# Two attention layers on one core: layer 1's scores between the halves of its head mixing, column strips for layer 0's row sums, and another order at an image's start

## The chip, the cores and the metric

The kernel runs on one core of one Trainium2 chip. The metric is the device time of one launch in microseconds (us). Before the change it is 4345.27 us, the median of three runs (4342.4 to 4345.67). All data are float32.

## What is computed

Eight images of 512 channels and 32 x 32 positions (T = 1024 tokens) pass two residual layers, each on a group-normalized input. Both layers are attention with 8 heads of 64 channels; layer 1 mixes the heads' scores before the softmax and normalizes the attention map afterwards. Cut to what matters:

```python
# layer 0, x: (8, 512, 1024) after group normalization
q, k, v = split(qkv_w @ groupnorm(x) + qkv_b)          # 8 heads of 64 channels
weight = softmax(einsum('bct,bcs->bts', q * s, k * s))
out = proj_w @ (x + weight @ v) + proj_b

# layer 1
attn = einsum('bhdq,bhdT->bhqT', q, k) * scale
attn = einsum('gh,bhqT->bgqT', w_head, attn)            # mixing of the heads
attn = softmax(attn)
attn = (attn - mean) / sqrt(var + eps) * gamma + beta   # over a head's whole map
out = (attn @ v) @ w_proj.T + b_proj
```

In both layers x = x + layer(groupnorm(x)).

## The kernel before

The program fixes the order of instructions by hand for every engine. Waits and buffers follow from the program: a pool hands out a fixed number of buffers per tag, and a new tile waits until its buffer's last reader is done.

Layer 0 runs image by image (b). In `attention0` 64 steps i go over 8 groups g (a pair of heads, half of the queries) and 8 blocks of keys. A step has `scores` (L982, 64 x 64 tiles of TensorE, four at a time), the exponential on ScalarE (L987), `values` (L1008) and `sums`, which adds up the exponentials on VectorE (L993, L995). After each group `totals` adds them over the keys with a matrix of ones (L1030), two engines copy the two results to a row (L1035, L1036) and two DMAs bring it into 128 partitions. `reciprocals` adds the two parts (L1045), inverts them and spreads them by DMA, and `finish` multiplies (L1068). An `Agenda` holds work for given steps: `totals` comes 2 steps after its group, `reciprocals` 6, `finish` 10 after. The statistics of the next image run beside (L620 and L631 are their small matmuls), and the projections (L856) stand between images.

Layer 1 goes over images again. Within one it goes over 32 half steps x, and 5 more to drain (`half_step`):

- `scores(x, i)`, i = 0, 1 (L1575): 8 matmuls, 16 instructions, of 64 x 64 x 256 into a PSUM tile `s`, copied to `raw` by VectorE (i = 0 and x odd or below 4, L1588) or ScalarE (L1590). Two half steps fill one tile t of `raw`.
- `regroup` (L1599): eight DMAs r of 256 KB per tile t, which put eight heads of one query row beside each other in `re`, in the order R_ORDER. In the steady part each is issued behind the end of a mix or of a values block. Up to half step 4 all are issued at the half step's end. `re` has two halves; one half holds the weights wv for `v_pair` at an image's start.
- `mix(y, j)` with y = x - 4 (L1623): 32 matmuls, 64 instructions, of 64 x 64 x 64 into a PSUM tile `m`, then the exponential (L1629).
- `values(w, i)` with w = x - 5 (L1669): 128 x 64 x 256, summed over a quarter of the image (8 half steps) and taken out by `leave` (L1689, L1691).
- `squares` on ScalarE (L1640), `sum_e` and `sum_e2` on VectorE (L1647, L1651); after each quarter `totals` (L1700) in 32-column strips, `reciprocals`, and `divide` (L1759).

TensorE's order in a half step is scores 0, mix 0, values 0, scores 1, mix 1, values 1. The tiles `s`, `m`, those of the projections and of `v_pair` share one pool of three buffers of two PSUM banks (`m_psum`). `pieces` are DMAs for the next image, one behind each scores block. `v_pair` (L1394) makes two token blocks of v: the image's last two pairs run at the ends of half steps 1 and 2. Each `Projection` (L1319) forms seven products in an ORDER; its `leave` adds them up and calls `finish` for the quarters (0,0), (1,1), (1,0), (0,1) of the result. The first two scores blocks read the upper half of the channels of q, that is quarters (0,0) and (0,1).

Of the kernel before, what the change touches and what calls it, by code (L numbers as in the profile page):

```python
# [9 lines left out]
F32 = mybir.dt.float32  # L10
# [457 lines left out]
def tile_two_attention_layers(  # L468
# [181 lines left out]
    with ExitStack() as l0:  # L650
# [9 lines left out]
        def small_psum(nm):  # L660
            return ps_a.tile([P, FB], F32, tag="small", name=nm)
# [308 lines left out]
        def attention0(b, agenda):  # L970
            q, k, v = q_t[b], k_t[b], v_t[b]
            e, acc, u, zacc, zc, rzb = {}, {}, {}, {}, {}, {}

            def scores(i):

                f, hp, kc = i // (NG * H // 2), i // NG % (H // 2), i % NG
                ps = score_psum(f"s0_{b}_{i}")
                for c in range(2):
                    for m in range(2):
                        r = slice(m * D, m * D + D)  # L980
                        k0 = kc * P + c * D
                        nc.tensor.matmul(  # L982
                            ps[c * D : c * D + D, m], k[r, hp, k0 : k0 + D], q[r, hp, ts(f, FB)],
                            start=True, stop=True,
                        )
                e[i] = epool.tile([P, 2, FB], F32, tag="e", name=f"e0_{b}_{i}")
                nc.scalar.activation(e[i], ps, AF.Exp, scale=S0 * S0)  # L987

            def sums(i):
                g, kc = i // NG, i % NG  # L990
                if kc == 1:
                    zacc[g] = zpool.tile([P, 2, FB], F32, tag="zacc", name=f"zacc_{b}_{g}")
                    nc.vector.tensor_add(zacc[g], e[i - 1], e[i])  # L993
                elif kc > 1:
                    nc.vector.tensor_add(zacc[g], zacc[g], e[i])  # L995

            def values(i):

                g, hp, kc = i // NG, i // NG % (H // 2), i % NG
                if kc == 0:  # L1000
                    acc[g] = [
                        ps_a.tile([P, FB], F32, tag=f"a{a}", name=f"a0_{b}_{g}_{a}", bufs=2 - a)
                        for a in range(2)
                    ]
                for a in range(2):
                    rows = slice(a * D, a * D + D)
                    for m in range(2):
                        nc.tensor.matmul(  # L1008
                            acc[g][a][m * D : m * D + D], v[rows, kc, ts(2 * hp + m, D)],
                            e[i][rows, m], start=(kc == 0), stop=(kc == NG - 1),  # L1010
                        )
                if kc == NG - 1:

                    u[g] = [
                        zpool.tile([P, FB], F32, tag=f"u{a}", name=f"u_{b}_{g}_{a}")
                        for a in range(2)
                    ]
                    for a in (1, 0):
                        nc.scalar.copy(u[g][a], acc[g][a])

            def totals(g):

                z = [
                    ps_a.tile([P, FB], F32, tag="a0", name=f"z_{b}_{g}", bufs=2),
                    small_psum(f"z_{b}_{g}_1"),
                ]
                for a in range(2):
                    rows = slice(a * D, a * D + D)
                    for m in range(2):
                        nc.tensor.matmul(  # L1030
                            z[a][m * D : m * D + D], ones[rows, :D], zacc[g][rows, m],
                            start=True, stop=True,
                        )
                row = zpool.tile([P, 2, FB], F32, tag="row", name=f"row0_{b}_{g}", bufs=1)
                nc.scalar.copy(row[:, 0], z[0])  # L1035
                nc.vector.tensor_copy(row[:, 1], z[1])  # L1036
                zc[g] = stat.tile([P, 2, T // P], F32, tag="zc", name=f"zc_{b}_{g}")
                for a in range(2):
                    nc.sync.dma_start(out=zc[g][:, a], in_=row[0::D, a])

            def reciprocals(g):

                nc.vector.tensor_add(u[g][0], u[g][0], u[g][1])
                zs = stat.tile([P, T // P], F32, tag="zs", name=f"zs_{b}_{g}")
                nc.vector.tensor_add(zs, zc[g][:, 0], zc[g][:, 1])  # L1045
                rz = stat.tile([P, T // P], F32, tag="rz0", name=f"rz_{b}_{g}")
                nc.vector.reciprocal(rz, zs)
                zd = dram.tile([2, FB], F32, tag=f"zd0_{b}_{g}", name=f"zd0_{b}_{g}")
                nc.sync.dma_start(out=zd, in_=rz)
                rzb[g] = zpool.tile([P, FB], F32, tag="rzb", name=f"rzb_{b}_{g}")  # L1050
                for m in range(2):
                    nc.sync.dma_start(
                        out=rzb[g][m * D : m * D + D], in_=zd[m].partition_broadcast(D)
                    )
                col = b * H + g
                junk = stat.tile([P, T // P], F32, tag="junk0", name=f"junkz_{b}_{g}")
                nc.vector.tensor_scalar(
                    junk, zs, 1.0, 0.0, ALU.mult, ALU.add, accum_out=chk[:, 1, col : col + 1]
                )
                r2 = stat.tile([P, T // P], F32, tag="r20", name=f"r2_{b}_{g}")  # L1060
                nc.vector.scalar_tensor_tensor(
                    r2, rz, 1.0 / RZ_MAX, rz, ALU.mult, ALU.mult,
                    accum_out=chk[:, 0, col : col + 1],
                )

            def finish(g):
                hp, f = g % (H // 2), g // (H // 2)
                nc.vector.tensor_mul(u[g][0], u[g][0], rzb[g])  # L1068
                dst = xa_t[b][:, hp, ts(f, FB)]
                nc.vector.tensor_add(dst, dst, u[g][0])  # L1070


            for i in range(0, NI + 2, 2):
                if i < NI:
                    scores(i)
                    scores(i + 1)
                if i >= 2:
                    for w in (i - 2, i - 1):
                        values(w)
                        sums(w)  # L1080
                    if (i - 1) % NG == NG - 1:
                        g = (i - 1) // NG
                        agenda.at(i + 2, lambda g=g: totals(g))
                        agenda.at(i + 6, lambda g=g: reciprocals(g))
                        agenda.at(i + 10, lambda g=g: finish(g))
                agenda.run(i)
                agenda.run(i + 1)
# [61 lines left out]
    with ExitStack() as l1:  # L1149
# [144 lines left out]
                nc.vector.tensor_sub(t[:, i], x, y)  # L1294

        class Projection:
            ORDER = (1, 6, 2, 7, 5, 4, 3)

            def __init__(self, nm, key, n, t, finish, begin=None):

# [257 lines left out]
        class Attention1:  # L1558
# [5 lines left out]
            def scores(self, x, i):  # L1564
# [15 lines left out]
                if x > MLAG:  # L1580
                    self.piece(last)
                if x % 2 and i == 1:
                    self.due = [(t, r) for r in R_ORDER]
                if x % 2 == 0 and i == 0:
                    self.raw[t] = rawpool.tile([P, H, 2, KB], F32, tag="raw", name=f"raw_{b}_{t}")
                dst = self.raw[t][:, 2 * hp : 2 * hp + 2]
# [22 lines left out]
                        behind(dma, ins)  # L1609
                self.pieces = self.pieces[n:]  # L1610

            def mix(self, y, j):

                t, kc = y // 2, y % 2
                if j == 0:
                    self.e[y] = epool.tile([P, 2, T], F32, tag="e", name=f"e1_{self.b}_{y}")
                ps = m_psum(f"m1_{self.b}_{y}_{j}")
                for r in R_ORDER:
                    for c in range(2):
                        k0 = kc * P + c * D  # L1620
                        for a in range(2):
# [4 lines left out]
                                wmix[rows].rearrange("p g i -> p (g i)"),  # L1626
                                start=True, stop=True,
                            )
                nc.scalar.activation(self.e[y][:, j], ps.rearrange("p a c -> p (a c)"), AF.Exp)  # L1629
                self.regroup(last)  # L1630

            def squares(self, y, j):
                if y % QLAG == 0:
# [86 lines left out]
            def reciprocals(self, qb, ag=None, x=None):  # L1720
# [7 lines left out]
                self.rzb = zpool.tile([P, T], F32, tag="rzb", name=f"rzb_{b}_{qb}")  # L1728
                rzb = self.rzb
                spread = [  # L1730
                    lambda two=two: nc.sync.dma_start(
                        out=rzb[two * D : two * D + D], in_=zd[two].partition_broadcast(D)
                    )
                    for two in range(2)
                ]
                if ag is None:
                    for fn in spread:
# [58 lines left out]
            def half_step(self, x, ag):  # L1796
                y, w = x - MLAG, x - MLAG - 1
                first = 0 < w < NX and w % QLAG == 0
                if first:

                    self.scores(x, 0)
                    self.leave(w // QLAG - 1)
# [10 lines left out]
                    self.sum_e2(w, 0)  # L1813
                    self.sum_e2(w, 1)
                if 0 <= y < NX:
                    self.mix(y, 0)
                if 0 <= w < NX:
                    self.values(w, 0)
                if x < NX:
                    self.scores(x, 1)  # L1820
                if 0 <= y < NX:
                    self.mix(y, 1)
                if x <= MLAG or x >= NX:
                    self.regroup(n=NR)
                if x >= NX:
# [28 lines left out]
        for b in range(B):  # L1854
            more = b + 1 < B
            a = Attention1(b)
            ag = Agenda()
            for i in range(NV):
                ag.at(1 + i, lambda i=i: v_pair(b, NV + i))
            free = (NX // 2 - 2 + b) % 2  # L1860
            if more:
                a.pieces += [lambda i=i: y_piece(b + 1, i) for i in range(4 * NCC)]
# [119 lines left out]
```

## Time and profile before

| what | value |
|---|---|
| median of three runs | 4345.27 us |
| the profiled execution | 4355.81 us |
| its span, first to last instruction | 4353.9 us |
| granted TensorE clock | 0.995 |
| TensorE matmuls busy | 4192.3 us |
| VectorE busy | 2911.7 us |
| ScalarE busy | 2329.9 us |
| mix: matmuls, and weight loads | 602.1 us, 585.4 us |
| scores and values of layer 1 | 558.4 us, 558.2 us |
| scores and values of layer 0 | 491.5 us, 485.0 us |
| sums of layer 0 (L1030) | 67.1 us |
| regroup DMAs | 1024 of 256 KB |

The profile lists instructions by line, engine and tile. A row of the timeline has the start and duration in us, the engine, line and operation, the tile written and read, the size (rows * columns of the array that are used, then partitions x elements), and in brackets the idle time before with what ended it; "issue" there means that no wait on another engine is on record. Matmuls overlap, so the distance from one start to the next tells more than a block's duration. PE is TensorE, PEld its weight loads, ACT ScalarE, DVE VectorE, SPq and POOLq the queues of SyncE and GpSimd.

### The profile page before, as it was taken

What the parts mean: (1) busy time and instruction counts of PE and PEld (TensorE: products, weight loads), DVE (VectorE), ACT (ScalarE), POOL (GpSimd) and SP (SyncE); (2) the same over time, 40 slices, a digit from 0 to 9 for tenths busy, and PEclk for the clock granted to TensorE, in tenths of its full rate; (3) what the DMA queues carried; (4) which work ended last, traced back from release to release, by engine and by line L of the source; (5) the groups of instructions that cost most, each with busy time, mean ns of one, the idle gap of its engine ahead of it and who ended that gap; (6) DMA issues with size and microseconds to landing.
All of it is one profiled execution on the core that took longest, in us unless ns stands there. A gap on an engine that the chain in (4) does not pass through costs nothing.

```text
span 4353.9 us, 131477 instructions
## 1 busy us (share of the span) xinstructions
PE 4192.3 (96%) x58568; PEld 2243.2 (52%) x58568; DVE 2911.7 (67%) x3881; ACT 2329.9 (54%) x2730; POOL 53.3 (1%) x86
## 2 busy tenths in 40 slices
PE   7999999999999999799999999999999999999998
PEld 4353535353535353356466466466466466465565
DVE  4748484848484848458668668568577578577577
ACT  1717171717171716158368278277187287286385
POOL 0000000000000000000000000000000000000000
PEclk9999999999999999899999999999999999999999
DMA  4213131212121211257367377277286286375474
GB/s 145 77 54 101 50 104 49 79 49 79 52 76 54 74 49 43 87 140 191 123 166 183 105 187 180 97 195 189 81 202 172 90 206 158 114 199 141 135 175 136
DMA packets 260464, 521.21 MB, mean 120 GB/s; under 512 B 58992, under 2 KB 66544, under 8 KB 253232
## 3 DMA queue, kind: packets, MB, share of 16 engines
q1 hardware_dynamic: 255008, 509.92, 41.8%
q8 instruction: 461, 7.55, 0.8%
q0 software_dynamic: 2576, 0.69, 0.3%
q10 hardware_dynamic: 2304, 2.10, 0.2%
q14 instruction: 115, 0.94, 0.1%
HBM read 196.11 MB, written 46.92 MB: 56 GB/s over the span
## 4 chain that ended last, share of the span: by engine, by line
PE 84%; DVE 6%; DMA 5%; ACT 2%; issue 2%; SPq 1%; POOL 0%; DVEq 0%; ACTq 0%; POOLq 0%
PE a L1669 11%; PE s L1575 11%; PE m L1623 10%; PE s L982 8%; PE a L1008 8%; PE pk L1319 5%; PE pq L1319 4%; PE pp_p L856 4%; PE pv_p L856 4%; PE pv L1394 4%; PE pk_p L856 4%; PE pq_p L856 4%; PE pp L1319 3%; DMA re<-raw 2%; PE t L1700 2%
## 5 line engine op out<-in xcount | busy, mean ns | idle before, releaser
L1623 PEld LDWEIGHTS m<-wmix,re 64*64 64x64 f32 x32768 | 585.4, 135 | 141.9 <-issue 73.7
L1623 PE MATMUL m<-wmix,re 64*64 64x64 f32 x32768 | 602.1, 219 | 44.0 <-issue 34.9
L987 ACT ACTIVATE e<-s 128x1024 f32<-128x1024 f32 x512 | 497.4, 1026 | 235.4 <-PE s L982 235.4
L1629 ACT ACTIVATE e<-m 128x1024 f32<-128x1024 f32 x512 | 528.2, 1032 | 157.7 <-PE m L1623 154.2
L1647 DVE TENSOR_TENSOR z<-z,e 128x1024 f32<-128x1024 f32 x448 | 538.9, 1218 | 69.8 <-ACT e L1629 69.6
L1651 DVE TENSOR_TENSOR z<-z,e 128x1024 f32<-128x1024 f32 x448 | 534.9, 1219 | 74.6 <-ACT e L1640 74.4
L1669 PE MATMUL a<-e,v 128*64 128x256 f32 x4096 | 558.2, 392 | 27.5 <-ACT q L1691 20.9
L1575 PE MATMUL s<-k,q 64*64 64x256 f32 x8192 | 558.4, 388 | 6.2 <-DVE q L1431 4.6
L1590 ACT COPY raw<-s 128x1024 f32<-128x1024 f32 x368 | 372.7, 1015 | 284.4 <-PE s L1575 245.8
L982 PE MATMUL s<-q,k 64*64 64x512 f32 x4096 | 491.5, 594 | 2.3 <-ACT e L987 2.3
L995 DVE TENSOR_TENSOR zacc<-zacc,e 128x1024 f32<-128x1024 f32 x384 | 468.2, 1219 | 28.6 <-ACT e L987 3.9
L1008 PE MATMUL a<-e,v 64*64 64x512 f32 x4096 | 485.0, 589 | 0.0
L1640 ACT ACTIVATE e<-e 128x1024 f32<-128x1024 f32 x448 | 462.1, 1063 | 0.0
L1575 PEld LDWEIGHTS s<-k,q 64*64 64x64 f32 x8192 | 271.5, 132 | 274.5 <-issue 170.7
L1669 PEld LDWEIGHTS a<-e,v 128*64 128x64 f32 x4096 | 250.6, 136 | 155.0 <-issue 24.9
L1008 PEld LDWEIGHTS a<-e,v 64*64 64x64 f32 x4096 | 159.9, 133 | 281.2 <-issue 281.2
L982 PEld LDWEIGHTS s<-q,k 64*64 64x64 f32 x4096 | 156.2, 133 | 281.5 <-issue 257.7
L1588 DVE COPY raw<-s 128x1024 f32<-128x1024 f32 x144 | 176.1, 1223 | 96.3 <-PE s L1575 84.7
L1394 PE MATMUL pv<-re,y 128*128 128x512 f32 x512 | 227.6, 598 | 0.0
L1394 PEld LDWEIGHTS pv<-re,y 128*128 128x128 f32 x512 | 94.8, 190 | 120.1 <-issue 120.1
L1399 DVE COPY v<-pv 128x512 f32<-128x512 f32 x32 | 22.1, 689 | 149.4 <-ACT v L1398 149.4
L856 PE MATMUL pv_p<-left_v,tmp 128*128 128x256 f32 x512 | 115.1, 383 | 4.2 <-DVE tmp L885 4.2
(285 smaller groups left out, 4133.0 us busy)
## 6 DMA issues: line engine op xcount, KB each, us to landing
re<-raw SPq DMA_DIRECT2D x1024, 256.0 KB
left_q<-left_q SPq DMA_DIRECT2D x17, 1792.0 KB
left_p<-left_p SPq DMA_DIRECT2D x17, 1792.0 KB
left_k<-left_k SPq DMA_DIRECT2D x10, 1792.0 KB
x<-in_x_dram SPq DMA_DIRECT2D x32, 512.0 KB
rzb<-zd SPq DMA_DIRECT2D x128, 128.0 KB
x<-x SPq DMA_DIRECT2D x64, 256.0 KB
rzb<-zd SPq DMA_DIRECT2D x64, 256.0 KB
```

The source lines that it names most:

```text
L856: nc.tensor.matmul(out, st, mv, start=start, stop=(k == 1), skip_group_check=True)
L982: nc.tensor.matmul(ps[c * D : c * D + D, m], k[r, hp, k0 : k0 + D], q[r, hp, ts(f, FB)], start=True, stop=True,)
L987: nc.scalar.activation(e[i], ps, AF.Exp, scale=S0 * S0)
L1008: nc.tensor.matmul(acc[g][a][m * D : m * D + D], v[rows, kc, ts(2 * hp + m, D)], e[i][rows, m], start=(kc == 0), stop=(kc == NG - 1),)
L1319: nc.tensor.matmul(self.ps[m][:, i], w[:, left, k * HC + i * P : k * HC + i * P + P], right[:, k], start=(k == 0 and m != 2), stop=(k == 1 ...
L1394: nc.tensor.matmul(ps[:, m], y_t[b][:, c, ts(2 * i + m, P)], w[:, c], start=(c == 0), stop=(c == NCC - 1),)
L1575: last = nc.tensor.matmul(pv[c * D : c * D + D, m, j], qo_t[b][r, 2 * qb + j, hp, ts(c, D)], k_t[b][r, hp, ts(kb, KB)], start=True, stop=True,
L1623: last = nc.tensor.matmul(ps[c * D : c * D + D, a, ts(r, D)], self.re[t, r][rows, j, k0 : k0 + D], wmix[rows].rearrange("p g i -> p (g i)" ...
L1629: nc.scalar.activation(self.e[y][:, j], ps.rearrange("p a c -> p (a c)"), AF.Exp)
L1647: nc.vector.tensor_add(self.z[:, j], self.z[:, j], self.e[y][:, j])
L1651: nc.vector.tensor_add(self.z2[:, j], self.z2[:, j], self.e2[j])
L1669: last = nc.tensor.matmul(self.acc[w][two * D : two * D + D, s].rearrange("p (c i) -> p c i", i=Q8), v_t[b][:, kc, ts(g, D)], e[:, g], sta ...
```

## The change

It has five parts. In layer 0 `totals` takes all 128 rows at once, in four strips of 32 columns with 256 queries each, into one PSUM tile; one copy of half the width and one DMA follow, and the addition of two parts goes. In layer 1 `mix` is cut in two halves of four rows r each, and the scores block stands between them: mix, scores, mix, values, and the same again. The mix tile is opened in the first half; the exponential and the regroup follow the second. A Projection forms its last two products in the order 3, 4. At an image's start the last `v_pair` runs in half step 3, before the regroups of that half step, and these go in the order 4 to 7, 0 to 3. The spreading of the reciprocals in layer 1 has four DMAs of 32 partitions in place of two of 64.

```diff
             def totals(g):
-                z = [
-                    ps_a.tile([P, FB], F32, tag="a0", name=f"z_{b}_{g}", bufs=2),
-                    small_psum(f"z_{b}_{g}_1"),
-                ]
-                for a in range(2):
-                    rows = slice(a * D, a * D + D)
-                    for m in range(2):
-                        nc.tensor.matmul(
-                            z[a][m * D : m * D + D], ones[rows, :D], zacc[g][rows, m],
-                            start=True, stop=True,
-                        )
-                row = zpool.tile([P, 2, FB], F32, tag="row", name=f"row0_{b}_{g}", bufs=1)
-                nc.scalar.copy(row[:, 0], z[0])
-                nc.vector.tensor_copy(row[:, 1], z[1])
-                zc[g] = stat.tile([P, 2, T // P], F32, tag="zc", name=f"zc_{b}_{g}")
-                for a in range(2):
-                    nc.sync.dma_start(out=zc[g][:, a], in_=row[0::D, a])
+                HB = FB // 2
+                z = ps_a.tile([P, FB], F32, tag="a0", name=f"z_{b}_{g}", bufs=2)[:, :HB]
+                for c in range(4):
+                    nc.tensor.matmul(
+                        z[c * 32 : c * 32 + 32], ones[:, :32], zacc[g][:, c // 2, ts(c % 2, HB)],
+                        start=True, stop=True, tile_position=(0, c * 32),
+                    )
+                row = zpool.tile([P, HB], F32, tag="row", name=f"row0_{b}_{g}")
+                nc.scalar.copy(row, z)
+                zc[g] = stat.tile([P, T // P], F32, tag="zc", name=f"zc_{b}_{g}")
+                nc.sync.dma_start(out=zc[g], in_=row[0::32])
             def reciprocals(g):
                 nc.vector.tensor_add(u[g][0], u[g][0], u[g][1])
-                zs = stat.tile([P, T // P], F32, tag="zs", name=f"zs_{b}_{g}")
-                nc.vector.tensor_add(zs, zc[g][:, 0], zc[g][:, 1])
+                zs = zc[g]
...
         class Projection:
-            ORDER = (1, 6, 2, 7, 5, 4, 3)
+            ORDER = (1, 6, 2, 7, 5, 3, 4)
...
                 if x % 2 and i == 1:
-                    self.due = [(t, r) for r in R_ORDER]
+                    order = (4, 5, 6, 7, 0, 1, 2, 3) if t == 1 else R_ORDER
+                    self.due = [(t, r) for r in order]
...
-            def mix(self, y, j):
+            def mix(self, y, j, half):
                 t, kc = y // 2, y % 2
-                if j == 0:
-                    self.e[y] = epool.tile([P, 2, T], F32, tag="e", name=f"e1_{self.b}_{y}")
-                ps = m_psum(f"m1_{self.b}_{y}_{j}")
-                for r in R_ORDER:
+                if half == 0:
+                    if j == 0:
+                        self.e[y] = epool.tile([P, 2, T], F32, tag="e", name=f"e1_{self.b}_{y}")
+                    self.m = m_psum(f"m1_{self.b}_{y}_{j}")
+                ps = self.m
+                for r in R_ORDER[4 * half : 4 * half + 4]:
...
-                nc.scalar.activation(self.e[y][:, j], ps.rearrange("p a c -> p (a c)"), AF.Exp)
-                self.regroup(last)
+                if half == 1:
+                    nc.scalar.activation(
+                        self.e[y][:, j], ps.rearrange("p a c -> p (a c)"), AF.Exp
+                    )
+                    self.regroup(last)
...
                 spread = [
-                    lambda two=two: nc.sync.dma_start(
-                        out=rzb[two * D : two * D + D], in_=zd[two].partition_broadcast(D)
+                    lambda i=i: nc.sync.dma_start(
+                        out=rzb[ts(i, 32)], in_=zd[i // 2].partition_broadcast(32)
                     )
-                    for two in range(2)
+                    for i in range(4)
                 ]
...
             def half_step(self, x, ag):
                 y, w = x - MLAG, x - MLAG - 1
                 first = 0 < w < NX and w % QLAG == 0
+                if 0 <= y < NX:
+                    self.mix(y, 0, 0)
                 if first:
...
                 if 0 <= y < NX:
-                    self.mix(y, 0)
+                    self.mix(y, 0, 1)
                 if 0 <= w < NX:
                     self.values(w, 0)
+                if 0 <= y < NX:
+                    self.mix(y, 1, 0)
                 if x < NX:
                     self.scores(x, 1)
                 if 0 <= y < NX:
-                    self.mix(y, 1)
+                    self.mix(y, 1, 1)
+                ag.run(x - 0.75)
                 if x <= MLAG or x >= NX:
                     self.regroup(n=NR)
...
-            for i in range(NV):
-                ag.at(1 + i, lambda i=i: v_pair(b, NV + i))
+            for i, slot in enumerate((1, 3 - 0.75)):
+                ag.at(slot, lambda i=i: v_pair(b, NV + i))
```

## The prediction, made before the changed kernel ran

> **What bounds the kernel now.** I read the page first, then the groups of instructions, then TensorE's own timeline in a layer 0 stretch, at the start of a layer 1 image and in its steady part, then ScalarE's timeline and a table of windows. The page:
>
> ```profile
> span 4353.9 us, 131477 instructions
> ...
> PE 4192.3 (96%) x58568; PEld 2243.2 (52%) x58568; DVE 2911.7 (67%) x3881; ACT 2329.9 (54%) x2730; POOL 53.3 (1%) x86
> ...
> q8 instruction: 461, 7.55, 0.8%
> ```
>
> TensorE sets the end, so only what shortens its own sequence or its waits counts. The queue line matters too: 461 packets of 16 KB (7.55 MB / 461) for 2 x 58568 TensorE instructions, one packet per 254 of them: these are TensorE's instruction refills. A steady stretch of layer 1, then its TensorE sequence:
>
> ```profile
> 2860.00:3020.00 160.00, 155.03 (x4369) 107.39 (x4372) 129.90 (x144) 137.28 (x153) 5.84 (x9) 1.00 0.78 193
> ```
> ```profile
> 2905.73 1.09 PE L1575 MATMUL s<-k,q 64*64 64x256 f32 x16
> 2906.65 1.11 PE L1623 MATMUL m<-wmix,re 64*64 64x64 f32 x64
> 2907.69 1.08 PE L1669 MATMUL a<-e,v 128*64 128x256 f32 x8
> 2908.70 0.66 PE L1575 MATMUL s<-k,q 64*64 64x256 f32 x8
> ```
>
> Read the starts: scores S 0.92, mix M 1.04, values V 1.01, so 2.97 us per half and 5.94 per half step (224 of these hold all parts). ScalarE is 86% busy there and VectorE 81%, both below TensorE. What breaks the rhythm:
>
> ```profile
> 2032.70 0.64 PE L1623 MATMUL m<-wmix,re 64*64 64x64 f32 x32
> 2034.11 0.69 PE L1623 MATMUL m<-wmix,re 64*64 64x64 f32 x32 [0.76 <-issue]
> 2034.73 1.08 PE L1669 MATMUL a<-e,v 128*64 128x256 f32 x8
> ```
>
> A mix stops half way with no semaphore named. Such stops stand at one place of every 256 TensorE instructions, and end at the earliest 1.4 us after a 16 KB packet: a refill that came late. Adding up the M starts to V starts over the whole trace (432 pairs, median 1.04, sum 541 us) leaves 92 us above the median: 60 in 72 refills, 23 in 24 waits for `leave` at a quarter's start (0.94 each), 10 in waits for regrouped scores. V and S hold 12 us of refills more, so refills cost 72 us.
>
> Layer 0, and the start of an image of layer 1:
>
> ```profile
> 836.30 1.90 PE L1008 MATMUL a<-e,v 64*64 64x512 f32 x16
> 838.02 1.04 PE L1030 MATMUL z<-zacc,ones 64*64 64x512 f32 x8
> 840.37 0.35 PE L620 MATMUL pm<-gs_m,gavg 128*128 128x4 f32 x2 [1.32 <-DVE gs_m L618]
> 840.66 1.95 PE L982 MATMUL s<-q,k 64*64 64x512 f32 x16
> 842.42 1.90 PE L1008 MATMUL a<-e,v 64*64 64x512 f32 x16
> 844.25 0.39 PE L631 MATMUL pv<-gs_sq,gavg 128*128 128x4 f32 x2
> ```
> ```profile
> 2818.55 0.65 PE L1575 MATMUL s<-k,q 64*64 64x256 f32 x4
> 2819.77 3.79 PE L1575 MATMUL s<-k,q 64*64 64x256 f32 x60 [0.57 <-DVE q L1431]
> 2823.49 7.13 PE L1394 MATMUL pv<-re,y 128*128 128x512 f32 x16
> 2830.56 1.96 PE L1575 MATMUL s<-k,q 64*64 64x256 f32 x32
> ...
> 2852.96 1.29 PE L1623 MATMUL m<-wmix,re 64*64 64x64 f32 x56
> 2855.09 0.34 PE L1623 MATMUL m<-wmix,re 64*64 64x64 f32 x8 [0.85 <-DMA re<-raw]
> ```
>
> The reader is to see a wait for q in the first scores, a wait for regrouped scores in the third mix pair, and in layer 0 the price of leaving the 64x64 tiling (below).
>
> **What the Trainium skill says.** "TensorEngine Tiling (Array Packing)", Key Properties: changing the tiling mode drains TensorE. The trace agrees: a block of 1.72 us takes 1.83 before a 128-row one (842.42 to 844.25), and M takes 1.04 before V but 0.94 before S. "Runtime: NRT & Kernel Launch", Instruction fetch mechanics: instructions come in blocks of 256 through a DMA queue, the crossing "mostly hidden". The trace agrees on the blocks; hidden it is in most crossings, but not for those 72 us.
>
> **The change, part by part.**
>
> *Layer 0 sums.* Now 8 matmuls of 512 columns in four tiles: z to the next s is 0.86 us (49 cases; 1.02 in the 8 between projections). New: 8 of 256 columns on four 32-column strips, two rounds of 0.214 (a round of four 512s takes 1.717/4 = 0.429): 0.43. The mode changes now: +0.11 before it, 0.14 inside (the layer 1 sums of this form, L1700, take 1.85 for four rounds, 1.71), +0.05 for the s after (842.42 - 840.66 = 1.76 against 1.72). 0.73, so 0.13 x 49 = 6. Between projections nothing switches: about 0.5 x 8 = 4. In 7 cases pm follows and waits for VectorE, which first does the row copy that goes (0.69, L1036); with a shorter path of the sums 0.85 x 7 = 6. Bounds: if z costs 0.86 as now, 8 in all; at best 24. I take -16. The strips might run one after the other (+56), but L1700's 16 matmuls in 1.85 exclude it. VectorE and ScalarE lose 1 us per sum, hidden now and later.
>
> *Mix in halves, TensorE's own time.* No instruction is added. A round of four mix pairs takes 0.058 throughout. V, M/2, S, M/2: the first half pays the 0.05 after V that S pays now (where V is followed by M directly, M takes 1.09, not 1.04), the second the 0.11 before V: 0.52 + 0.87 + 0.58 + 1.01 = 2.97, as now. Price 0.
>
> *Refills.* A refill is asked for as TensorE enters a block and usable 3.9 us later (median of 313; 2.9, 3.5, 4.4, 5.0 at 10, 25, 75, 90%). A half step's half has 128 + 16 + 32 = 176 instructions, so 256 are a half and 80 more. Now these 80 can lie all in M: by position 256 last 3.62 (four of eleven positions) to 5.16 us. In the new order 3.92 to 4.55. The mean shortfall against the measured spread is 0.28 us now (87 us in 313; the trace has 72) and 0.21 after: 65, scaled 54. I take -18, the ends 0 (the delay follows the DMA load, a 0.78 share) and -40.
>
> *PSUM buffers, the added wait.* Three buffers serve four tiles per half step, and a freed buffer is handed on in the order in which buffers come free (the compiled kernel before: product 5 of a projection takes product 6's buffer, not that of the older product 1). Mix tiles are now opened before the scores but freed after them. So the second scores get the buffer of the first scores of the same half step, once its copy to raw is done; before they had a whole half step. The copy starts 1.16 us after the scores' start when its engine is idle (2914.85 to 2916.01 below) and takes 1.02 on ScalarE, 1.22 on VectorE: done at 2.2 or 2.4; the second scores start at 2.97. Slack 0.8 and 0.6. Behind that wait on TensorE stand M/2 and V, and exp and squares wait for them.
>
> ```profile
> 2916.01 1.02 ACT L1590 COPY raw<-s 128x1024 f32<-128x1024 f32 x1 [1.06 <-PE s L1575]
> 2916.94 1.02 ACT L1629 ACTIVATE e<-m 128x1024 f32<-128x1024 f32 x1
> ```
>
> ScalarE's order (square, copy, square, exp, copy, exp) is unchanged, some 5.5 us of 5.94 in even half steps, and is free when the copy comes. Copies wait for a regroup DMA some 2 times per image by 0.4 to 1.7 us; the scores now come 0.5 later behind that DMA, so only the longest reach through: +3 (0 to 12). At x = 4 and 5 no values separate the blocks: between scores and second scores only 0.93 us of mix lie, the copy needs 1.3: 0.75 x 8 = +6 (3 to 9).
>
> *Start of an image.* The second v_pair moves from the end of half step 2 to that of 3 with its two copies; TensorE's work is the same, but 7 us now lie between the second raw tile and its mixing. Its eight regroups are issued before v_pair ends for rows 4 to 7, after it for 0 to 3, which overwrite wv; SP holds nothing urgent behind them, and these four have 10 us until half step 6 against about 6 (8 took about 11 us, 2 MB at 190 GB/s). The 10 us of mix waits go: -9 (5 to 12).
>
> *ORDER.* Four scores at the start take 4.94 us from first start to pv; two take 1.89, so 1.17 is wait. The first scores need q's quarter (0,1), now ready one product earlier; the last quarter is needed by the third: -1.0 x 8 = -8 (5 to 10). For the output projection nothing changes.
>
> *rzb* in four pieces instead of two takes one half step more of DMA slots and lands a half step before the division: 0, its cover the more than 6 us to half step x + 6; without it 1 us in 24 cases. At the image's end the four issues (0.57 each) delay SP's xs loads by 1 us, which wait longer than that for TensorE.
>
> **Sum.** -16 -18 +3 +6 -9 -8 = -42. The profiled execution took 4355.8 (span 4353.9 and 1.9 around it), so 4314; the median of the three runs is 10.5 lower, so 4303.
>
> **Rivals.**
> A (0.23): the refill delay grows with the denser traffic or stays, saving 0: 4345 - 24 = 4321. For: delay's spread comes from the queue, not the order. Against: the shortest blocks go.
> B (0.09), slower: the second scores wait for exp, not for the copy. In even half steps ScalarE reaches the end of exp 4.0 us after the first scores' start, 1.05 after the second could start: x 112 = 120; the next scores wait 0.17 for the second exp, x 224 = 38. Refills then hide (-54): 4345 + 158 - 54 - 24 = 4425. It decides as soon as the copy is over 0.8 us late. Against: the order of frees.
> C (0.10): the smoother order covers nearly all refills: -55 for -18: 4266.
> Main 0.58.
>
> **Numbers.** The main case's own range is 4280 to 4328. What a measurement of this kernel tells from no change is 0.2%, 9 us. Main, A and C are nearly all faster: 0.84; 0.06 within, from the weak ends of A; 0.10 slower, B and a little of A. Range 4266 to 4338.
>
> **What would show it.** z blocks with 128x256 matmuls, 0.7 us to the next s, pm's idle near 0.5. In the steady part S 0.87, M halves 0.52 and 0.58, half step 5.94. Refill stops under 55 us. No idle before a mix from regroups at half step 6; four first scores in 3.9 us. Wrong: idle of over 0.2 us before every second scores, released by ScalarE; refill stops as many as now.

## The result, and the profile after

The changed kernel takes 4285.86 us, the median of four runs (4282.67 to 4293.95), against 4344.5 of the kernel before on the same chip: a ratio of 0.9868, 95% interval 0.9851 to 0.9885. That is 59 us less by the medians, 57 (50 to 65) by the ratio. The profiled execution lies at its median; that of the kernel before lay 11 us above its own, so of the 69.5 us between the two spans some 11 belong to that one execution.

The page of the changed kernel. TensorE still sets the end, and fetches as many instructions as before:

```profile
span 4284.4 us, 131340 instructions
...
PE 4167.7 (97%) x58568; PEld 2219.1 (52%) x58568; DVE 2862.4 (67%) x3753; ACT 2312.0 (54%) x2730; POOL 53.4 (1%) x86
...
q8 instruction: 461, 7.55, 0.7%
```

A steady stretch of layer 1, TensorE's timeline after. From start to start: first half of the mix 0.51, scores 0.87, second half 0.57, values 1.02, so 2.97 us per half and 5.94 per half step, as before:

```profile
2908.08 0.69 PE L1621 MATMUL m<-wmix,re 64*64 64x64 f32 x32
2908.59 1.05 PE L1569 MATMUL s<-k,q 64*64 64x256 f32 x16
2909.46 0.64 PE L1621 MATMUL m<-wmix,re 64*64 64x64 f32 x32
2910.03 1.08 PE L1670 MATMUL a<-e,v 128*64 128x256 f32 x8
2911.05 0.69 PE L1621 MATMUL m<-wmix,re 64*64 64x64 f32 x32
```

Where the 69.5 us between the two traces lie (end of layer 0; per image, first scores to the totals of the first quarter; the two quarters that follow; the rest):

| stage | before to after |
|---|---|
| layer 0 (its end at 1794.3, now 1765.2) | -29.1 us |
| start and first quarter, sum of eight images | 631.4 to 603.0, -28.4 us |
| second and third quarter | -13.3 us |
| rest | +1.3 us |

The second row holds most of what belongs to one execution. In e_l0, e_l0act and e_l0dve (below), whose layer 1 is that of the kernel before, it is 624.0, 620.6 and 625.5 us; a second profile of the changed kernel has 608.7.

The waits of TensorE by what ended them (in total, times, longest), before, and then after:

```profile
PE m L1623 <- issue: 34.9, 51, 2.3
...
PE a L1669 <- ACT q L1691: 20.9, 24, 0.9
...
PE m L1623 <- DMA re<-raw: 7.9, 14, 1.1
```
```profile
PE a L1670 <- ACT q L1692: 20.8, 24, 0.9
...
PE m L1621 <- issue: 8.3, 17, 1.0
PE m L1621 <- DMA re<-raw: 6.3, 11, 1.1
...
PE s L1569 <- ACT raw L1586: 3.0, 13, 0.2
```

Stops of the mix with no semaphore fall from 35 to 8 us. They are the instruction refills: nearly all stand at one place of every 256 TensorE instructions. A new wait, scores for ScalarE's copy to raw, shows as 3 us of idle time. At first sight this says that the halves of the mix did most of it. The experiments say otherwise.

Two places that the prediction named, in TensorE's timeline after. Layer 0 at a new image's statistics (pm without a wait), and an image's start up to half step 5:

```profile
826.75 0.64 PE L1027 MATMUL z<-zacc,ones 128*32 128x256 f32 x8
827.32 0.39 PE L620 MATMUL pm<-gs_m,gavg 128*128 128x4 f32 x2
827.63 1.95 PE L982 MATMUL s<-q,k 64*64 64x512 f32 x16
```
```profile
2772.32 1.96 PE L1569 MATMUL s<-k,q 64*64 64x256 f32 x32
2774.64 2.14 PE L1569 MATMUL s<-k,q 64*64 64x256 f32 x32 [0.36 <-DVE q L1425]
2776.71 7.13 PE L1388 MATMUL pv<-re,y 128*128 128x512 f32 x16
...
2795.84 1.11 PE L1621 MATMUL m<-wmix,re 64*64 64x64 f32 x64
2797.20 1.09 PE L1569 MATMUL s<-k,q 64*64 64x256 f32 x16 [0.24 <-ACT raw L1586]
2798.11 1.11 PE L1621 MATMUL m<-wmix,re 64*64 64x64 f32 x64
2799.42 1.09 PE L1569 MATMUL s<-k,q 64*64 64x256 f32 x16 [0.20 <-ACT raw L1586]
```

Below, "excess" of a block is the distance from its start to the next block's start, less the median of all blocks of its kind and neighbours in that trace, put down to what stands at the longest gap in it ("refill" where that is the place of a refill). Summed over layer 1's mix, scores and values blocks, refill excess is 66 us before and 20.5 after.

### The profile page after: what moved, and what is told of

It is laid out like the page before. It is cut to its first block, busy times and chain, and to the rows that moved or that the text cites. A ratio compares the mean times of both kernels' runs of the same rounds, so it can differ in the third digit from the quotient of the medians.

```text
span 4284.4 us, 131340 instructions
## 1 busy us (share of the span) xinstructions
PE 4167.7 (97%) x58568; PEld 2219.1 (52%) x58568; DVE 2862.4 (67%) x3753; ACT 2312.0 (54%) x2730; POOL 53.4 (1%) x86
## 4 chain that ended last, share of the span: by engine, by line
PE 89%; DVE 5%; ACT 3%; DMA 2%; issue 1%; SPq 0%; DVEq 0%; ACTq 0%
PE m L1621 12%; PE a L1670 11%; PE s L982 10%; PE a L1008 10%; PE s L1569 9%; PE pk L1313 5%; PE pq L1313 4%; PE pp_p L856 4%; PE pv_p L856 4%; PE pv L1388 4%; PE pk_p L856 4%; PE pq_p L856 4%; PE pp L1313 3%; PE t L1701 2%; DMA re<-raw 1%
## 5 line engine op out<-in xcount | busy, mean ns | idle before, releaser
L1621 PEld LDWEIGHTS m<-wmix,re 64*64 64x64 f32 x32768 | 622.1, 134 | 289.0 <-issue 153.9
L1621 PE MATMUL m<-wmix,re 64*64 64x64 f32 x32768 | 691.5, 221 | 15.3 <-issue 8.3
L1670 PE MATMUL a<-e,v 128*64 128x256 f32 x4096 | 556.2, 392 | 23.4 <-ACT q L1692 20.8
L1569 PE MATMUL s<-k,q 64*64 64x256 f32 x8192 | 538.7, 378 | 7.4 <-ACT raw L1586 3.0
```

The source lines that it names most:

```text
L1569: last = nc.tensor.matmul(pv[c * D : c * D + D, m, j], qo_t[b][r, 2 * qb + j, hp, ts(c, D)], k_t[b][r, hp, ts(kb, KB)], start=True, stop=True,
L1621: last = nc.tensor.matmul(ps[c * D : c * D + D, a, ts(r, D)], self.re[t, r][rows, j, k0 : k0 + D], wmix[rows].rearrange("p g i -> p (g i)" ...
L1670: last = nc.tensor.matmul(self.acc[w][two * D : two * D + D, s].rearrange("p (c i) -> p c i", i=Q8), v_t[b][:, kc, ts(g, D)], e[:, g], sta ...
```

## The experiments

Each changes one part and was timed beside the kernel before on the same chip. Ratios are to that kernel (median 4346.4 or 4348.4 us beside them); "us less" is worked out from ratio and interval.

| run | what differs | median us | ratio, 95% interval | us less |
|---|---|---|---|---|
| e_mix44 | before + halves of the mix | 4349.28 | 0.9999, 0.999 to 1.0007 | 0 (-3 to 4) |
| e_mix26 | before + mix cut 2 and 6 | 4348.23 | 0.9995, 0.9988 to 1.0002 | 2 (-1 to 5) |
| e_mix80 | before + whole mix ahead of the scores | 4430.15 | 1.0181, 1.0164 to 1.0198 | -79 (-86 to -71) |
| e_l0 | before + strips of layer 0 | 4314.79 | 0.9914, 0.9898 to 0.9929 | 37 (31 to 44) |
| e_l0act | before, both row copies on ScalarE | 4338.84 | 0.9981, 0.9974 to 0.9987 | 8 (6 to 11) |
| e_l0dve | e_l0, row copy on VectorE | 4324.06 | 0.9947, 0.9933 to 0.996 | 23 (17 to 29) |
| e_start | before + later v_pair, other regroup order | 4332.19 | 0.9972, 0.9964 to 0.998 | 12 (9 to 16) |
| e_ord | before + ORDER | 4341.73 | 0.9992, 0.9983 to 1.0 | 3.5 (0 to 7) |
| e_nomix | after without halves of the mix | 4288.25 | 0.9869, 0.9854 to 0.9883 | 57 (51 to 63) |
| e_after | the changed kernel again | 4289.37 | 0.9872, 0.9857 to 0.9886 | 56 (50 to 62) |
| e_best | after + earlier leave | 4272.43 | 0.9837, 0.9824 to 0.985 | 71 (65 to 76) |
| e_best2 | e_nomix + earlier leave | 4266.23 | 0.9817, 0.9804 to 0.9831 | 80 (73 to 85) |

**Are the halves of the mix worth anything?** `e_mix44` has only `mix` and `half_step` of the change; `e_mix26` cuts the rows 2 and 6; `e_mix80` puts all eight ahead of the scores.

```diff
-                for r in R_ORDER[4 * half : 4 * half + 4]:
+                for r in (R_ORDER[2:] if half else R_ORDER[:2]):     # e_mix26
+                for r in (() if half else R_ORDER):                  # e_mix80
```

> The kernel before with the mix halves alone (4 rows before the scores, 4 after). The refill theory (R: late instruction refills fall because the burst of 128 mix instructions is cut): the refill stops in layer 1 fall from some 70 us to under 25, and the time by 35 to 45 us after 6 us for the two waits at half steps 4 and 5. If the prediction's term had the right size (-18 refills, +9 waits), only -9. The rival O (the mix simply stands earlier, so that exponentials and regroups have more room): also -35 to -45, so this run alone does not tell R from O.

> The kernel before with the mix cut 2 to 6 (2 rows before the scores, 6 after). R: 96 mix instructions stay in one piece, two of eleven places of a refill still have only 3.6 us for 256 instructions: about half of the gain of the cut 4 to 4, -15 to -25 us, refill stops 35 to 50 us. O: the same as the cut 4 to 4.

> The kernel before with the whole mix, uncut, ahead of the scores (mix, scores, values). R: the burst of 128 is still there, refill stops stay at 60 to 80 us, time within 8 us of before (0 to +6 for the buffers). O: the mix stands as early as with the halves or earlier, so -35 to -45 us.

The first two come out at the time of the kernel before: the theory in which covered refills carry the gain (R) misses, the rival that the mix only has to stand earlier (O) misses too, and so does the prediction's -9. Yet the stops did fall. Refill excess is 43 us in e_mix44 and 48 in e_mix26; in the five kernels with the old order in layer 1 (before, e_l0, e_l0act, e_l0dve, e_ord) it is 66, 50, 52, 62 and 54, mean 57. Some 9 to 14 us are gained, a rough size, as each is one profile and the five spread over 16. In e_mix44 they are given back by the scores' waits for the copies to raw, of which the kernel before has none over 0.15 us, and by many small delays with no semaphore (excess of the latter 6.5 us, before 3.5). Of TensorE's waits in e_mix44:

```profile
PE m L1625 <- issue: 23.7, 35, 2.0
...
PE s L1575 <- ACT raw L1590: 3.4, 15, 0.2
...
PE s L1575 <- DVE raw L1588: 1.6, 9, 0.2
```

Where e_mix26 gives them back was not worked out. e_mix80 shows how far this goes wrong; neither R nor O saw it coming. TensorE's waits in its profile, which is of its slowest execution (17 us above its median):

```profile
PE m L1625 <- DMA re<-raw: 53.9, 83, 2.0
PE s L1575 <- ACT e L1632: 24.7, 30, 0.9
```

The mix now meets regroups that have not landed (54 us, 8 before), and scores wait for a buffer that the exponential holds: the mechanism of the slower rival B, at 30 places and not at the 112 and 224 that it counted. Refill stops fall there as well, to some 33 us, though the mix is uncut and the kernel slower: fewer of them are no sign of a gain.

The same question from the other end: the changed kernel with the mix undivided, beside the changed kernel itself.

```diff
-                for r in R_ORDER[4 * half : 4 * half + 4]:
+                for r in R_ORDER:
...
-                if 0 <= y < NX:
-                    self.mix(y, 0, 0)
...
                 if 0 <= y < NX:
-                    self.mix(y, 0, 1)
+                    self.mix(y, 0)
```

> The changed kernel without the mix halves (mix uncut, after the scores, as before); all its other parts are in. Theory A (parts add up, and the mix halves are worth 0 as they were alone): the same as the changed kernel within 4 us. Theory I (the halves pay only together with the new start, which takes their cost at half steps 4 and 5 or their refills away): 8 to 20 us slower than the changed kernel.

> The changed kernel itself again, beside its variants on one chip: -55 to -62 us against before. Its profile shows by how much the refill stops of one kernel differ from one execution to another: within 8 us of the 20 us of its first profile.

Their intervals all but coincide: worth nothing here too, within the 8 us or so that these two can tell apart (e_mix44, with 0 (-3 to 4), is closer). TensorE's mix waits in e_nomix, beside 8.3 and 6.3 in the changed kernel:

```profile
PE m L1618 <- issue: 18.2, 35, 1.5
...
PE m L1618 <- DMA re<-raw: 3.1, 7, 1.2
```

Refill excess is 36 us in e_nomix and 20.5 and 23 in the two profiles of the changed kernel, so 13 to 15 are saved. Against them stand the waits for the copies at half steps 4 and 5 (6.5 us by the distances of starts, worked out further down), 3 more of waits for regroups (6.1 to 9.7 and 9.1; in the last image's drain one mix lost 3.4 us where e_nomix lost 1.6), and 4 to 6 of small delays (2.3 to 6.6 and 8.5), whose cause the traces do not name.

**Where do the 37 us of layer 0 come from?** `e_l0` is the change of `totals` and `reciprocals` alone.

> The kernel before with layer 0's sums in column strips alone. Theory W (most of the gain is the wait of the statistics' small matmul for the row copy on VectorE, which goes): -25 to -30 us, pm's idle time at 0 as in the changed kernel. Theory Z (the price of the sums themselves): -6 to -10 us. The prediction had -16.

More than twice the predicted 16, and more than the 25 to 30 of theory W. The distance from the sums (z) to pm, which the prediction took to lose 0.85, falls from 2.0 to 3.6 us to 0.57 in each of the seven cases: 18.2 to 4.0 us. The strips do three things at once there: VectorE loses its row copy, the sums' way to rzb gets shorter, and the second z tile is gone, which used the one PSUM buffer that pm and pv use (`small_psum`). Two runs take these apart.

```diff
-                nc.vector.tensor_copy(row[:, 1], z[1])        # e_l0act, on before
+                nc.scalar.copy(row[:, 1], z[1])
-                nc.scalar.copy(row, z)                        # e_l0dve, on e_l0
+                nc.vector.tensor_copy(row, z)
```

> The kernel before with one edit: both row copies of layer 0's sums are done by ScalarE, one after the other; the sums themselves stay eight matmuls of 512 columns. It asks where most of the 35 us of the strips come from. W1 (VectorE's row copy of 0.69 us stands ahead of pm's copy in the seven cases where a projection's mean follows the sum): taking only that copy off VectorE brings 5 us or more, 4341 or less. W2 (the way of the sums, row to zc to reciprocal to rzb, ends earlier with the strips, and VectorE no longer waits for rzb ahead of pm's copy): that way is one ScalarE copy longer here, about 0.7 us, so no gain, 4344 to 4352.

> The kernel before with the strips for layer 0's sums, but the one row copy that is left is done by VectorE instead of ScalarE. W1 (VectorE's row copy ahead of pm's copy is the cost): part of the gain of the strips is lost, about half of 0.69 x 7 and the rest of VectorE's queue, 4322 to 4330. W2 (the earlier end of the way of the sums is the gain): as with ScalarE's copy, 4311 to 4318.

VectorE's timeline of the kernel before at the z of 838.02 that the prediction shows: a wait for the spread reciprocals, two operations, the row copy, and only then the copy that pm needs.

```profile
838.13 0.69 DVE L1068 TENSOR_TENSOR u<-u,rzb 128x512 f32<-128x512 f32 x1 [2.33 <-DMA rzb<-zd]
838.86 0.69 DVE L1070 TENSOR_TENSOR xa<-xa,u 128x512 f32<-128x512 f32 x1
839.47 0.68 DVE L1036 COPY row<-z 128x512 f32<-128x512 f32 x1
840.07 0.16 DVE L618 COPY gs_m<-mv 128x4 f32<-128x4 f32 x1
```

e_l0act, three timelines at the same place: VectorE, then TensorE, then ScalarE.

```profile
832.85 0.16 DVE L618 COPY gs_m<-mv 128x4 f32<-128x4 f32 x1
```
```profile
833.49 1.04 PE L1030 MATMUL z<-zacc,ones 64*64 64x512 f32 x8
835.69 0.38 PE L620 MATMUL pm<-gs_m,gavg 128*128 128x4 f32 x2 [1.16 <-ACT row L1036]
```
```profile
834.57 0.59 ACT L1035 COPY row<-z 128x512 f32<-128x512 f32 x1 [1.34 <-PE z L1030]
835.05 0.59 ACT L1036 COPY row<-z 128x512 f32<-128x512 f32 x1
```

pm's data are there before z even starts (832.85); in the other six cases they are there 0.4 us or more before pm. Still pm starts 2.20 us after z in all seven: it waits until the second z tile is copied out of its PSUM buffer. In the kernel before this wait was there as well, under the name of the later one, VectorE's. e_l0dve has no such tile, but a row copy on VectorE; its VectorE and TensorE:

```profile
830.34 0.42 DVE L1032 COPY row<-z 128x256 f32<-128x256 f32 x1 [1.36 <-PE z L1027]
830.68 0.16 DVE L618 COPY gs_m<-mv 128x4 f32<-128x4 f32 x1
```
```profile
829.63 0.64 PE L1027 MATMUL z<-zacc,ones 128*32 128x256 f32 x8
830.90 0.39 PE L620 MATMUL pm<-gs_m,gavg 128*128 128x4 f32 x2 [0.62 <-DVE gs_m L618]
```

In five of the seven VectorE is idle, but a row copy that waits for z stands ahead of gs_m: pm starts 1.26 to 1.67 us after z, 9.6 us in the seven. Both expectations of W1 hold in number, and those of W2 do not, but W1 is not all. Of the 14.2 us at pm, the copy alone off VectorE gives 2.8 (18.2 to 15.4), and put back onto VectorE it takes 5.6 (4.0 to 9.6). For the 11.4 that are left there is an estimate: had pm in e_l0act waited for gs_m alone, it would have come some 8 us after z in the seven together. So the PSUM buffer holds some 7, and at most 4 are left for the shorter way. Part of the 7 is e_l0act's own, as its second copy starts 0.48 us behind the first on ScalarE. The other 5 us of e_l0act (7 in its trace) lie where VectorE was late behind these places: the scores after pm (15.6 to 12.4 us for the seven) and the last image's end (3.9). In the changed kernel gs_m is ready at 826.21, before z starts at 826.75:

```profile
824.71 0.69 DVE L1062 TENSOR_TENSOR u<-u,rzb 128x512 f32<-128x512 f32 x1 [0.64 <-DMA rzb<-zd]
825.44 0.69 DVE L1064 TENSOR_TENSOR xa<-xa,u 128x512 f32<-128x512 f32 x1
826.05 0.16 DVE L618 COPY gs_m<-mv 128x4 f32<-128x4 f32 x1
```

The wait for rzb is shorter there (0.64, not 2.33; over layer 0 VectorE waits 56 us for it, 94 before). The shorter way alone wasn't run, so its share stays an estimate.

**The start of an image.** `e_start` has the later v_pair and the order of its regroups, `e_ord` only ORDER.

> The kernel before with the start of an image alone: the last v_pair in half step 3 and the regroups of the second raw tile in the order 4 to 7, 0 to 3. Theory S (the long v_pair now stands just ahead of the first mixes, so regroups and instruction refills catch up under it): -15 to -22 us, the idle time by refills before the first quarter's totals down from 17 us to under 6. The prediction's term: -9, regroup waits alone.

> The kernel before with only the changed order of the first half steps' projection products. The prediction's term: 1.0 x 8 = 8 us less, 4339. By the trace of the changed kernel only 0.56 x 8 = 4.5 us less, 4342. By what the runs so far leave over for it: some 10 us less, 4337.

TensorE's idle time from first scores to the first quarter's totals, summed over eight images: waits for regroups fall from 6.5 us to 1.3 in e_start, refill stops from 16.8 to 8.7 (12 to 17 in the kernels with the old start and the mix undivided). So it is more than the regroup waits of the prediction's term, but less than theory S with its 15 to 22 us and stops under 6. The later v_pair and the other order were not run apart. e_ord's four scores take 4.38 us to the first v_pair, 4.94 before: 0.56 x 8 = 4.5, and 3.5 (0 to 7) is measured, neither the prediction's 8 nor the 10 that seemed left over.

**A better version.** The largest wait left in the list above is for `leave`: a quarter's first values wait 0.87 us until ScalarE has copied out the sums of the last quarter. TensorE at one such place in the changed kernel, ScalarE's timeline there, and then ScalarE's in e_best:

```profile
2853.20 1.08 PE L1670 MATMUL a<-e,v 128*64 128x256 f32 x8 [0.87 <-ACT q L1692]
```

```profile
2851.17 0.58 ACT L1710 COPY row<-t 128x512 f32<-128x512 f32 x1 [2.12 <-DVE row L1709]
2851.65 1.50 ACT L1692 COPY q<-a 64x256 f32<-64x256 f32 x4
```
```profile
2842.49 1.03 ACT L1628 ACTIVATE e<-m 128x1024 f32<-128x1024 f32 x1
2843.41 1.50 ACT L1692 COPY q<-a 64x256 f32<-64x256 f32 x4
2845.64 0.59 ACT L1710 COPY row<-t 128x512 f32<-128x512 f32 x1 [0.74 <-DVE row L1709]
```

The copies, though their data are complete, stand behind a row copy that waits 2.12 us for the totals. e_best issues ScalarE's half of them right behind the last values:

```diff
+                        if qb < NQB - 1:
+                            self.leave(qb, (0,))     # ScalarE's half
                         self.totals(qb)
...
-                    self.leave(w // QLAG - 1)
+                    self.leave(w // QLAG - 1, (1,))  # VectorE's half
```

> The changed kernel with ScalarE's half of leave moved from the next half step to right behind the quarter's last values, ahead of the copy of the sums. If the 0.9 us wait of values at a quarter's start comes from leave queued behind that copy on ScalarE, it goes in 24 cases: -18 to -23 us against the changed kernel. If values then wait for something else, less.

> The changed kernel with the mix undivided as before, and with ScalarE's part of leave right behind a quarter's last values. If the halves of the mix are worth nothing also once the wait for leave is gone: 4271, as with the halves (4272). If the halves save refill stops that nothing else then covers (15 us in the traces): 4280 or more.

The wait is gone from both traces (20.8 us). By the table, 15 us are won against e_after, somewhat less than the 18 to 23 expected, and 23 with the mix undivided against e_nomix (these two did not run beside each other). e_best2 is the fastest kernel of this study, 4266 us. It did not run beside e_best either and their intervals overlap, so that it is the better one is not shown; that the halves bring no gain is.

## Why the prediction was right or wrong

The direction was right, and the time 17 us under the forecast and inside its range. That it came so near is in part luck: layer 0 brought about twice its term, and this cancelled the terms of the halves and of ORDER, of which little or nothing came. Term by term:

- **Layer 0, -16: right in kind, less than half in size.** The strips behave as worked out: the block before them takes 0.11 longer and that after 0.05, z itself 0.569 where 0.858 stood, so 0.13 per group. (That changing the tiling mode drains TensorE is what the Trainium skill, "TensorEngine Tiling (Array Packing)", Key Properties, says; it gives no price.) Between projections it is 0.31, not 0.5. The term that failed is pm: "0.85 x 7 = 6". It is 14.2. The prediction let some 0.5 us of idle time stay at pm, and none stayed: 2.35 to 0.57 in its own example is 1.78, or 12.5 in seven; the rest is that the seven go up to 3.6. And it named one releaser, VectorE's row copy; e_l0act shows the second under it, a PSUM buffer that z and pm share. And VectorE's lateness went on after pm: the scores behind pm gain 3.2 us more, and the last image's end some 5. Together with the 6.3 and 2.2 of the strips this is 31, less 0.8 that the blocks before z cost in the seven cases; in e_l0's trace layer 0 ends 29.9 us earlier. The runs of e_l0 measure 37 (31 to 44), so some 7 are in no place that the traces name.
- **Mix in halves, TensorE's own time, 0: right.** 0.51 + 0.87 + 0.57 + 1.02, the 0.52, 0.87, 0.58 and 1.01 of the forecast.
- **Refills, -18: near.** The excess falls by 13 to 15 (e_nomix against the changed kernel), 9 to 14 on the kernel before. The base was too high: 72 us came from one execution (66 as counted here), and kernels with the same layer 1 order have 50 to 66. Counted again, the earliest stop ends 1.2 us after its packet, not 1.4.
- **PSUM buffers, +6 and +3: the first right, the second too small.** At half steps 4 and 5 each second scores block starts 0.4 us late (1.36 and 1.31 from the mix before it, 0.93 without a wait): 0.4 x 16 = 6.5. The order in which buffers come free was read rightly: nowhere in the changed kernel do scores wait for exp. But "only the longest reach through: +3" left out that the mix's first half meets regroups earlier, 3 us more, and the small delays, 4 to 6, whose cause stays open. So the -9 of the two terms together became 0, which both pairs of runs show.
- **Start of an image, -9: right in size (12, 9 to 16), by half from elsewhere.** Waits for regroups give 5; the rest goes with refill stops, which fall by 4 to 8 there too. Why they do was not settled.
- **ORDER, -8: too large.** The first scores no longer wait, as said, but the third wait for the last quarter of q for 0.36 us; the step "the last quarter is needed by the third" was stated and given no cost. So the four take 4.38 us, not 3.9. 3.5 (0 to 7) measured, 4.5 in the trace.
- **rzb, 0:** not run alone. The parts run alone give 37 + 12 + 3.5 + 0 = 53, all together 56 to 59, each with 3 to 7 of uncertainty, so no effect of it or of a joint action shows.

Of the rivals, A (refills save nothing) had the wrong reason for a right consequence: the halves are worth nothing, not because stops stay but because what they save is spent. B's mechanism appears only if the whole mix goes ahead of the scores. C, nearly all refills covered, did not come: 20 us of them stay, and that the time lies halfway to C's 4266 is layer 0's doing.

## What to carry to other kernels

A wait that the profile gives to one releaser may have others just under it: list all that the waiting instruction needs (data, buffer, its producers' queues), over all its cases and not the one example, before pricing what goes when one of them does. A drop in one kind of stop isn't a gain until a run with that part alone says so; here 14 us of refills paid for 14 us of new small waits. And copies whose data are complete shouldn't stand in a queue behind one that still has to wait.

## What the runs showed of the hardware

- Refill stops differ between executions of one TensorE sequence: 50 to 66 us of excess over layer 1 in profiles of five kernels that share it (e_ord but for the order of two products), 20.5 and 23 in two of the changed kernel. The Trainium skill, "Runtime: NRT & Kernel Launch", Instruction fetch mechanics, calls the crossing mostly hidden; in number it is: of 371 crossings in layer 1, 85 cost more than 0.15 us before and 41 after. But 20 us stay even in the changed kernel, single ones up to 1.0 us in the mix (2.3 before).
- Four strips of 32 columns with all 128 rows run side by side: from the first of the eight instructions to the next block it is 0.57 us before scores of 64 x 64 and before the small pm of 128 x 128, and 0.71 before a projection of 128 x 128. Two rounds of 256 columns account for 0.43 (by the rate of the sums before, 0.858 for two rounds of 512), so 0.14 remain for leaving the strips. Why a projection takes 0.14 more was not settled.
